# Six parts of 51, 62, 73, 73, 73 and 71 edge groups in place of 73, 73, 73, 73, 62 and 49, in a graph attention layer on one Trainium2 core

## The chip, the cores and the metric

The kernel runs on one NeuronCore of one Trainium2 chip. The metric is the device time of one execution in microseconds. Three runs of the kernel before gave 5107.2, 5124.87 and 5132.39 us, so the median is 5124.87 us. Engines are named as in the profile: PE (matrix engine), PEld (its weight loads), DVE (vector), ACT (scalar), POOL (GpSimd) and SP (which only issues DMAs here).

## The reference

The layer has 12,500 nodes with 128 features and 412,500 directed edges with 64 features each. `dst` is sorted; `src` is not.

```python
h = x @ Wn + bn
q = x @ Wq + bq; k = x @ Wk + bk; v = x @ Wv + bv
eh = edge_attr_64 @ We + be
attn_in = concatenate([q[src], k[dst], eh], -1)
hmid = leaky_relu(attn_in @ A1 + b1, 0.2)
scores = leaky_relu(hmid @ A2 + b2, 0.2)          # 8 heads
w = softmax(scores.mean(-1), axis=0)               # over all edges
out = segment_sum(w[:, None] * v[dst], src, num_segments=12500)
y = layernorm(h + out) * gamma + beta
return layernorm(x + y)
```

The first layer is linear, so its products are folded: each edge needs one row of a table from its source node (`q A1`), one from its destination (`k A1` and `v`), and the product of its own features.

## The kernel before, in words

**Groups, blocks, tiles.** The edges are cut in the order of `dst` into 403 groups of 1024 (8 tiles of 128). The nodes are dealt into 98 blocks of 128 by their number modulo 98, so that each block gets about the same number of edges as a source. The work has two halves. The first, `make` (L749), takes the edges in the order of `dst`, forms for each edge one record of 260 floats (the sum of the destination's row and the edge's product, the row of `v`, and the place of the source in its block), and scatters it to a row of a DRAM table `rtab` that belongs to the block of its source. The second, `sums_of` (L980), reads the records back block by block, adds the source's row, computes the scores, keeps a running maximum for the softmax, and adds up `w * v` for the block's nodes.

**Parts.** The 403 groups are cut into six parts by `CUTS` (L34): 73, 73, 73, 73, 62 and 49 groups. Each part has its own number of tiles of room per block (`plan.tiles`, L61): 7, 7, 7, 7, 6 and 5. Two tables `rtab` alternate. The loop at L1568 emits, for p from 0 to 6, the instructions of `make(p)` interleaved evenly with those steps of the sums that deal with part p - 1; in part 0 the tables of the nodes (`tables`, L1495) and the preparation of the edge lists (`later`, L1547) stand in the place of the sums, packed into the first nine tenths of the part (`n0`, L1575). After part 5 nothing is left to make: the sums of the last part run alone, and then `closing` (L1314) normalises the rows. The order of the instructions on each engine is the order in which this loop emits them, and each engine runs its own in order.

**make, for one group.** SP loads `eat` (edge features), `dstb` and `kvs` four groups ahead (`load`, L754). PE and DVE count how many earlier edges go to each block (L785 to L836), which gives each edge its row. PE forms the records of four tiles in one PSUM tile `pkv` (L854, L860); ACT moves them out into a tile `rec` (L871, L872; six buffers); POOL issues one indirect DMA per tile (L883), so eight per group. A `rec` buffer is free again when its four scatters have landed.

**Filling.** Rows of a block that no record reaches must hold zeros before they are read. `fill` (L513) yields pieces for both tables: in each block the rows from the least count that can be expected up to the table's room of seven tiles. `fill_piece` (L526) writes them on SP from an SBUF tile `empty` (L508). In part 0 the pieces of the first table stand before group 40 (`plan.gate`, L76), those of the second in the rest of the nine tenths: 44 pieces of 780 KB and 54 of 520 KB.

**sums_of.** A unit is two blocks of one part: 14, 12 or 10 tiles; there are 49 units a part. Each unit's work is dealt into numbered steps (L1273 to L1305), and step numbers decide the order of emission. A unit's hidden layer takes two steps for each four tiles (`nk`), from step `s0`; the next unit's `s0` is `2 * nk` later (L990), so 8 steps for a unit of 14 tiles and 6 for 12 or 10. `e` (L987) is 1 for units of 14 tiles: it puts one or more steps between a DMA, or an operation on one engine, and the next one that needs it (the spread of the sources' row `rowB`, L1062; `biased`, `leaky_scores`, `heads`, L1290 to L1292; `reference`, L1295). For units of 12 and 10 tiles `e` is 0. `load` (L1012) reads a unit's records into one of six buffers `rt`. `heads` allocates `psm` (two PSUM buffers), which is freed by `total` (L1251) of the unit two before. `starts[p]` is the step of the first load of part p; the loop emits the steps up to `starts[p] - HOLD` (7) in the part before (L1574).

Of the kernel before, what the change touches and what calls it, by code (L numbers as in the profile page):

```python
# [10 lines left out]
FP = mybir.dt.float32  # L11
# [9 lines left out]
P = 128  # L21
# [9 lines left out]
XA = 3  # L31
SPAN = 42
NP = 6
CUTS = 0, 0.1811, 0.3623, 0.5434, 0.7246, 0.8784, 1  # L34
TABS = 2
WIDTH = 14
HOLD = 7
LATE = 3
R = 4
WR = 260  # L40
# [3 lines left out]
class Plan:  # L44
# [4 lines left out]
    def __init__(self, n, e, nb, groups):  # L49
        self.n, self.e, self.nb, self.groups = n, e, nb, groups  # L50
        cut = [round(groups * c) for c in CUTS]
        self.parts = list(zip(cut[:-1], cut[1:]))
# [400 lines left out]
def sorted_path(  # L453
# [8 lines left out]
    nc = tc.nc  # L462
    nb = plan.nb
# [6 lines left out]
    dram = ctx.enter_context(tc.tile_pool(name="dram", bufs=1, space=DRAM))  # L470
# [31 lines left out]
        nc.vector.memset(headsum[32 * j : 32 * j + 32, j : j + 1], 1.0)  # L502


    fmax = max(max(f) for f in plan.fill)
    empty = None

    def empties(pool):  # L508
        nonlocal empty
        empty = pool.tile([P, fmax, WR], FP, name="empty")  # L510
        nc.vector.memset(empty, 0.0)

    def fill(k, n):  # L513

        cap = plan.cap
        b = 0
        while b < nb:
            m = 1
            while m < n and b + m < nb and plan.fill[k][b + m] == plan.fill[k][b]:
                m += 1  # L520
            f = plan.fill[k][b]
            if f:
                yield b, m, f
            b += m

    def fill_piece(k, b, m, f):  # L526
        cap = plan.cap
        piece = nc.sync.dma_start(
            out=rtab[k][b * cap : (b + m) * cap, :]
            .rearrange("(b c) w -> b c w", b=m)[:, cap - f * P : cap, :]  # L530
            .rearrange("b (p k) w -> p b (k w)", p=P),
            in_=empty[:, :f, :]
            .rearrange("p (o k) w -> p o (k w)", o=1)
            .to_broadcast([P, m, f * WR]),
        ).ins
        if k == 0:
            tc.declare_no_dep(piece, group="rows0", reason="rows that no record has reached")
            tc.add_to_no_dep_group("fill0", piece)

# [28 lines left out]
    with tc.tile_pool(name="prep", bufs=1) as prep, tc.tile_pool(  # L568
        name="pprep", bufs=1, space=PSUM
# [103 lines left out]
    def spans():  # L673

        lim = const.tile([P, 2], FP)
        for i, (op, most) in enumerate(((ALU.max, SPAN - 1.0), (ALU.min, 0.0))):
            nc.vector.tensor_reduce(lim[:, i : i + 1], mm[:, i, :], AX.X, op)
            sign = 1.0 if op == ALU.max else -1.0
            nc.vector.tensor_scalar(
                bad[:, i : i + 1], lim[:, i : i + 1], sign, -sign * most, op0=ALU.mult, op1=ALU.add  # L680
            )
# [16 lines left out]
        out=above, in_=above, compare_op=ALU.is_gt, fill=0.0, base=0,  # L698
# [281 lines left out]
    def sums_of(bp):  # L980


        plans, s0, first, free, done, starts = [], 19, None, [], [], {}
        for p, bs, t in units:
            nt = len(bs) * t
            nk = -(-nt // 4)
            L, e = 2 * nk, int(nk > 3)  # L987
            turn = 11 if e else 8
            if plans:
                s0 += 2 * plans[-1][1]  # L990


            load_at = free[-BLKS] + 1 if len(free) >= BLKS else 0
            lead = turn + 8 if p in starts or p == 0 else turn + 8 + LATE
            s0 = max(s0, load_at + lead - 1)
            if first is not None:
                s0 = max(s0, first - (L + 5 + 3 * e))
            if len(done) > 1:
                s0 = max(s0, done[-2] + 1 - (L + 4 + 2 * e))
            f = s0 + L + 5 + 3 * e  # L1000
            load_at = max(load_at, s0 - lead)
            free.append(f + 3 + e + L)
            done.append(f + 4 + e + L)
            first = f + L
            starts.setdefault(p, load_at)
            plans.append((nt, nk, s0, load_at, f, e, turn))
        steps = {}

# [264 lines left out]
        for i, (nt, nk, s0, load_at, f, e, turn_at) in enumerate(plans):  # L1273
# [7 lines left out]
            for k in range(nk):  # L1281
                c = 4 * k
                n, s = min(4, nt - c), s0 + 2 * k
# [15 lines left out]
            for j, t0 in enumerate(range(0, nt, 4)):  # L1299
                n = min(4, nt - t0)  # L1300
# [6 lines left out]
        closing(bp, do, tail, f + 3 + e, f + 5 + e + 2 * j + 4)  # L1307
        order = lambda at: [(fn, args) for _, fn, args in sorted(at, key=lambda x: x[0])]
        return [order(steps.get(s, [])) for s in range(max(steps) + 1)], [
            starts[p] for p in range(NP)  # L1310
        ]


    def closing(bp, do, s0, s1, s2):  # L1314
# [164 lines left out]
        for name, bufs in (("xq", 2), ("nq", 1), ("eq", 1))  # L1479
    )  # L1480
    empties(np_)

    def parts3(to, rest, half):
# [63 lines left out]
    def later():  # L1547

        for c in range(1, len(chunks)):
            yield from edges(tmp, c, CH // 2)  # L1550
            yield

    def covered():

        most = np_.tile([1, G], FP, name="most")
        g = 0
        while g < G:
            h = g
            while h < G and ready.get(h, ng) == ready.get(g, ng):
                h += 1  # L1560
            nc.vector.memset(most[:, g:h], float(3 * NB * P * ready.get(g, ng) - P))
            g = h
        nc.vector.tensor_tensor(most, start, most, op=ALU.subtract)
        nc.vector.tensor_reduce(bad[0:1, 2 + 2 * NP : 3 + 2 * NP], most, AX.X, ALU.max)

    with tc.manual_schedule():
        done = 0
        for p in range(NP + 1):  # L1568
            a = make(p) if p < NP else iter(())
            na = 6 * (plan.parts[p][1] - plan.parts[p][0]) if p < NP else 0  # L1570
            if p == 1:
                steps, starts = sums_of(pool("blk", BLKS))
            here = done
            until = 0 if p == 0 else starts[p] - HOLD if p < NP else len(steps)  # L1574
            n0 = na * 9 // 10  # L1575
            fills = []
            if p == 0:
                i0 = 0
                for k, i1 in enumerate((6 * plan.gate - 12, n0)):
                    pieces = list(fill(k, 2))  # L1580
                    fills += [
                        (i0 + (i1 - i0) * j // len(pieces), (k, *piece))
                        for j, piece in enumerate(pieces)
                    ]
                    i0 = i1
            fills = fills[::-1]
            tabs, made, nt = tables() if p == 0 else iter(()), 0, 1 + (2 * ng - 1) * (NB + 7)
            more, sent, ne = later() if p == 0 else iter(()), 0, 11 * (len(chunks) - 1)
            for i, _ in enumerate(a):
                while fills and fills[-1][0] <= i:  # L1590
                    fill_piece(*fills.pop()[1])
                while made < nt and made * n0 < i * nt:
                    next(tabs, None)
                    made += 1
                while sent < ne and sent * n0 < i * ne:
                    next(more, None)
# [90 lines left out]
```

## Time and profile before

The profiled execution took 5108.98 us; its span, from the first to the last instruction, is 5107.2 us.

| | busy us | share of the span |
|---|---|---|
| PE | 4197.8 | 82% |
| DVE | 3989.1 | 78% |
| POOL | 3347.9 | 66% |
| ACT | 3275.2 | 64% |
| PEld | 3121.7 | 61% |

These shares are means over stages with different contents, so the profile is best read by stage. The stages can be found without any mark in the program: L883 issues eight scatters per group, so a stretch that holds 8 x 73 = 584 of them is one part of 73 groups. By this count the parts of `make` run from 65 to 870, to 1640, 2407, 3174, 3878 and 4482 us; the sums of the last part run until about 4975 us, and the closing until 5107 us. A stage's table gives, for each engine, the busy time in the stretch and in brackets the number of instructions; PEclk is the granted clock as a share of the full one, and then follow the busy share of the 16 DMA engines and the rate.

### The profile page before, as it was taken

Reading aid. Unit: us, or ns where it says so; the run is one execution under the profiler, and the core shown is the slowest. Engines: PE = TensorE matmul, PEld = TensorE weight load, DVE = VectorE, ACT = ScalarE, POOL = GpSimd, SP = SyncE. Lnnn points to the kernel's source line nnn. Section 1 sums busy time; section 2 is a strip of 40 time slices with the busy share of each in tenths; the row PEclk is TensorE's granted clock in tenths of the full one; section 3 lists DMA queues with packets and bytes.
Section 4 is the critical chain, followed back from the end, with each engine's and each line's share of the span. In section 5 each row is a group of like instructions: output and inputs, shape, how many; then the busy total and the mean of one; then the engine's idle time right before and its main releaser. Section 6 shows DMA issues by size and latency. Waiting matters only on the chain.

```text
span 5107.2 us, 97900 instructions
## 1 busy us (share of the span) xinstructions
PE 4197.8 (82%) x32676; PEld 3121.7 (61%) x32676; DVE 3989.1 (78%) x10011; ACT 3275.2 (64%) x8487; POOL 3347.9 (66%) x3265
## 2 busy tenths in 40 slices
PE   4556564998998989998999998999999899988880
PEld 2333332666766767776766776677777676666660
DVE  7666663888887888888888887888888788766678
ACT  2333331666766777776777776777777677766776
POOL 3777777777777777777777777777767566611002
PEclk7666665999999999999999999999999999999995
DMA  5889895988888998998988998998998898878763
GB/s 188 281 277 314 292 336 175 323 297 296 298 302 278 316 316 308 316 304 297 322 310 306 314 314 286 315 318 311 318 316 301 291 307 305 293 248 265 247 232 139
DMA packets 589700, 1477.77 MB, mean 289 GB/s; under 512 B 102746, under 2 KB 315629, under 8 KB 587392
## 3 DMA queue, kind: packets, MB, share of 16 engines
q1 hardware_dynamic: 434224, 1042.03, 62.4%
q0 software_dynamic: 154752, 429.39, 22.0%
q8 instruction: 259, 4.24, 0.3%
q14 instruction: 257, 2.11, 0.1%
q10 hardware_dynamic: 208, 0.00, 0.0%
HBM read 890.36 MB, written 580.68 MB: 288 GB/s over the span
## 4 chain that ended last, share of the span: by engine, by line
DMA 35%; PE 19%; POOL 16%; DVE 14%; issue 9%; ACT 7%; SPq 1%; ACTq 0%; DVEq 0%; POOLq 0%
DMA rtab<-rec,idx 18%; POOL rtab L883 16%; DMA row<-slT 6%; DMA rt<-rtab 5%; PE psm L1246 4%; DMA rowB<-row 4%; PE ph L1094 3%; PE pkv L860 3%; ACT rec L871 2%; PE ph L1085 2%; ACT ohw L1217 2%; PE pkv L854 2%; DVE hm L1109 2%; PE psm L1155 2%; PE psc L1122 1%
## 5 line engine op out<-in xcount | busy, mean ns | idle before, releaser
L883 POOL DMA_INDIRECT rtab<-rec,idx x3224 | 3287.0, 1020 | 1190.9 <-issue 789.4
L871 ACT ACTIVATE rec<-pkv 128x1024 f32<-128x1024 f32 x806 | 821.6, 1019 | 1125.1 <-DMA rtab<-rec,idx 789.5
L1217 ACT ACTIVATE ohw<-ohs,w 128x128 f32<-128x128 bf16 x3822 | 1259.5, 400 | 13.2 <-PE psm L1246 1.4
L1246 PE MATMUL psm<-rt,ohw 128*128 128x128 f32 x7644 | 1150.3, 293 | 8.9 <-ACT ohw L1217 7.5
L1246 PEld LDWEIGHTS psm<-rt,ohw 128*128 128x128 f32 x7644 | 983.5, 198 | 104.2 <-ACT hm L1105 31.3
L1105 ACT ACTIVATE hm<-ph 128x512 f32<-128x512 f32 (+1 forms) x1078 | 583.4, 541 | 473.3 <-PE ph L1094 466.8
L854 PE MATMUL pkv<-kvs,ohd 128*128 128x256 bf16 x3224 | 550.0, 299 | 402.9 <-ACT rec L871 378.9
L1094 PE MATMUL ph<-ohT,qs 128*128 128x512 bf16 (+3 forms) x4116 | 819.6, 321 | 39.6 <-DVE ohT L1074 39.4
L1109 DVE TENSOR_TENSOR hm<-ph,hm 128x512 f32<-128x512 f32 (+1 forms) x1078 | 668.0, 620 | 114.9 <-ACT hm L1105 114.5
L860 PE MATMUL pkv<-WeS,eat 64*128 64x128 f32 x6448 | 658.7, 329 | 0.0
L854 PEld LDWEIGHTS <-ohd 128*128 128x128 bf16 x3224 | 321.8, 105 | 542.2 <-issue 453.1
L1085 PE MATMUL ph<-ident,rt 128*128 128x128 f32 x3822 | 622.5, 281 | 14.3 <-DVE hm L1109 13.5
L1074 DVE TENSOR_SCALAR ohT<-rowB,iotaP 128x512 bf16<-128x512 uint8 (+1 forms) x1078 | 521.8, 484 | 119.3 <-DMA rowB<-row 114.3
L860 PEld LDWEIGHTS pkv<-WeS,eat 64*128 64x128 f32 x6448 | 487.9, 213 | 201.1 <-issue 199.0
L1094 PEld LDWEIGHTS <-qs 128*128 128x128 bf16 x4116 | 395.3, 100 | 173.4 <-issue 50.8
L1085 PEld LDWEIGHTS ph<-ident,rt 128*128 128x128 f32 x3822 | 477.2, 152 | 22.5 <-DVE hm L1109 17.9
L823 DVE TENSOR_TENSOR ats<-pc,oh 128x792 f32<-128x792 f32 x403 | 392.3, 973 | 106.1 <-PE pc L805 103.5
L1203 DVE TENSOR_TENSOR ohs<-iotaE,sl 128x512 bf16<-128x512 bf16 (+1 forms) x1078 | 415.0, 385 | 51.2 <-ACT ohw L1217 50.3
L1155 PE MATMUL psm<-headsum,z 128*128 128x4 f32 (+1 forms) x2156 | 286.4, 254 | 146.0 <-DVE z L1145 65.7
L834 DVE TENSOR_REDUCE pos<-ats 128x8 f32<-128x792 f32 x403 | 389.9, 967 | 3.4
L1155 PEld LDWEIGHTS psm<-headsum,z 128*128 128x128 f32 (+1 forms) x2156 | 273.9, 198 | 176.9 <-DVE z L1145 79.1
L1122 PE MATMUL psc<-hm,A2s 128*32 128x512 f32 (+3 forms) x2352 | 319.5, 533 | 12.8 <-DVE slT L1053 7.0
(151 smaller groups left out, 4080.8 us busy)
## 6 DMA issues: line engine op xcount, KB each, us to landing
rt<-rtab SPq DMA_DIRECT2D x196, 1820.0 KB
eat<-in_ea SPq DMA_DIRECT2D x201, 512.0 KB
rt<-rtab SPq DMA_DIRECT2D x49, 1560.0 KB
rt<-rtab SPq DMA_DIRECT2D x49, 1300.0 KB
qs<-qtab SPq DMA_DIRECT2D x294, 192.0 KB
rtab<-rec,idx POOLq DMA_INDIRECT x3224
dstb<-dtab SPq DMA_DIRECT2D x201, 256.0 KB
rowB<-row SPq DMA_DIRECT2D x196, 224.0 KB
```

What stands on the lines that cost most here:

```text
L854: nc.tensor.matmul(pk[:, h, i, :], ohd[:, t * P : (t + 1) * P], kvs, start=(i == 0), stop=False,)
L860: nc.tensor.matmul(pk[:, h, i, :D], eat[h * DE : (h + 1) * DE, (j + i) * P : (j + i + 1) * P], WeS[h * DE : (h + 1) * DE, :], start=False, ...
L871: nc.scalar.activation(rec[:, :, :, : 2 * D], pk, AF.Copy)
L883: one_tile = nc.gpsimd.indirect_dma_start(out=rtab[p % TABS][:, :], out_offset=bass.IndirectOffsetOnAxis(ap=idxs[g][:, t : t + 1], axis=0) ...
L1074: nc.vector.tensor_scalar(st["oh"][k][:, : n * P], st["rowB"][:, t0 * P : (t0 + n) * P], iotaP, None, op0=ALU.is_equal,)
L1085: nc.tensor.matmul(ph[:, j * P : (j + 1) * P], st["rt"][:, t0 + j, :D], ident, is_transpose=True, start=(j == 0), stop=False,)
L1094: nc.tensor.matmul(ph[:, cols], st["qs"][:, j0 // t, s, :], oh[:, cols], start=False, stop=(s == 2 and j1 == t0 + n),)
L1105: nc.scalar.activation(hm, state[i]["ph", k][:, : n * P], AF.Copy, scale=SLOPE)
L1109: nc.vector.tensor_tensor(hm, ph[:, : n * P], hm, op=ALU.max)
L1155: nc.tensor.matmul(st["psS"][:, t0 + j : t0 + j + (nv - 1) * sw + 1 : sw], z[: 32 * nv, j * P : (j + 1) * P], headsum[: 32 * nv, :nv], sta ...
L1217: nc.scalar.activation(ohw[:, j, :], ohs[:, :, j], AF.Copy, scale=st["w"][:, t0 + j : t0 + j + 1])
L1246: nc.tensor.matmul(st["psS"][:, (1 + u) * P : (2 + u) * P], ohw[:, j, :], st["rt"][:, t0 + j, D : 2 * D], start=(k == 0), stop=(k == t - 1),)
```

## The change

The parts become 51, 62, 73, 73, 73 and 71 groups, with room for 5, 6, 7, 7, 7 and 7 tiles per block; both the number of tiles (3822) and that of the units (294) stay. In part 0 the fill now covers each table only up to the room of the part that uses it first (two tiles per block and table: 98 pieces of 520 KB). The rows above are zeroed while the sums of that part are read: in part 1 two tiles per block of the first table (49 pieces of 520 KB), in part 2 one tile per block of the second (49 pieces of 260 KB). These late pieces are copied from a small DRAM tensor `zeros`, since `empty` lies in a pool that is closed after part 0; `zeros` is written once at the start. Units of 12 and 10 tiles get `e = 1` and eight steps when they are not of the last part, and their sources are turned 12 steps ahead rather than 8. The steps of a part end at the larger of `starts[p] - HOLD` and one past the last load of the part before.

```diff
-CUTS = 0, 0.1811, 0.3623, 0.5434, 0.7246, 0.8784, 1
+CUTS = 0, 0.1266, 0.2804, 0.4615, 0.6427, 0.8238, 1
...
+    zeros = dram.tile([P, fmax, WR], FP, name="zeros")
...
         nc.vector.memset(empty, 0.0)
+        nc.sync.dma_start(out=zeros, in_=empty)
...
     def fill(k, n):
-        cap = plan.cap
-        b = 0
+        b, top = 0, plan.tiles[k]
         while b < nb:
...
-            f = plan.fill[k][b]
-            if f:
-                yield b, m, f
+            a = plan.cap // P - plan.fill[k][b]
+            if a < top:
+                yield b, m, a, top - a
             b += m
 
+    def fill_top(k, n):
+        top, most = plan.tiles[k], plan.cap // P
+        if top < most:
+            for b in range(0, nb, n):
+                yield b, min(n, nb - b), top, most - top
...
-            .rearrange("(b c) w -> b c w", b=m)[:, cap - f * P : cap, :]
+            .rearrange("(b c) w -> b c w", b=m)[:, a * P : (a + f) * P, :]
...
-            in_=empty[:, :f, :]
+            in_=(empty if source is None else source)[:, :f, :]
...
-            L, e = 2 * nk, int(nk > 3)
-            turn = 11 if e else 8
+            L, e = 2 * nk, int(nk > 3 or p < NP - 1)
+            turn = (11 if nk > 3 else 12) if e else 8
             if plans:
-                s0 += 2 * plans[-1][1]
+                s0 += 2 * plans[-1][1] if not plans[-1][5] else max(8, 2 * plans[-1][1])
...
             starts.setdefault(p, load_at)
+            ends[p] = load_at
...
-            starts[p] for p in range(NP)
+            max(starts[p] - HOLD, ends[p - 1] + 1) if p else 0 for p in range(NP)
...
-            until = 0 if p == 0 else starts[p] - HOLD if p < NP else len(steps)
+            until = 0 if p == 0 else starts[p] if p < NP else len(steps)
...
+            if 0 < p <= TABS:
+                pieces = list(fill_top(p - 1, 2))
+                fills = [
+                    (na // 8 + na * j // (2 * len(pieces)), (p - 1, *piece, zeros))
+                    for j, piece in enumerate(pieces)
+                ]
```

More of the change, by code (lines that the diff above doesn't have):

```diff
@@ L502, in sorted_path @@
         nc.vector.memset(headsum[32 * j : 32 * j + 32, j : j + 1], 1.0)
-    fmax = max(max(f) for f in plan.fill)
+    fmax = max(
+        max(plan.tiles[k] - plan.cap // P + max(plan.fill[k]), plan.cap // P - plan.tiles[k])
+        for k in range(TABS)
+    )
+    zeros = dram.tile([P, fmax, WR], FP, name="zeros")
     empty = None
@@ L520, in fill, with fill_piece @@
                 m += 1
-            f = plan.fill[k][b]
-            if f:
-                yield b, m, f
+            a = plan.cap // P - plan.fill[k][b]
+            if a < top:
+                yield b, m, a, top - a
             b += m
-    def fill_piece(k, b, m, f):
+    def fill_top(k, n):
[3 more added lines that the diff above has]
+                yield b, min(n, nb - b), top, most - top
+    def fill_piece(k, b, m, a, f, source=None):
         cap = plan.cap
@@ L535, in fill_piece @@
         ).ins
-        if k == 0:
+        if k == 0 and source is None:
             tc.declare_no_dep(piece, group="rows0", reason="rows that no record has reached")
@@ L980, in sums_of @@
     def sums_of(bp):
-        plans, s0, first, free, done, starts = [], 19, None, [], [], {}
+        plans, s0, first, free, done, starts, ends = [], 19, None, [], [], {}, {}
         for p, bs, t in units:
```

## The prediction

> **What bounds the kernel now.** The page comes first: no engine is busy throughout, so shares of the whole say little.
>
> ```profile
> span 5107.2 us, 97900 instructions
> PE 4197.8 (82%) x32676; PEld 3121.7 (61%) x32676; DVE 3989.1 (78%) x10011; ACT 3275.2 (64%) x8487; POOL 3347.9 (66%) x3265
> ```
>
> The second view is the table of stretches, cut where the count of POOL instructions reaches eight per group (584 is 73 groups; two or so at an edge are counted twice).
>
> ```profile
> core 0: us, PE busy (x) PEld busy (x) DVE busy (x) ACT busy (x) POOL busy (x), PEclk, DMA share, GB/s
> 0.00:65.00 65.00, 12.77 (x44) 9.21 (x44) 40.58 (x81) 2.41 (x3) 2.95 (x14) 0.66 0.30 93
> 65.00:870.00 805.00, 457.51 (x2452) 298.24 (x2453) 503.82 (x960) 265.50 (x377) 620.19 (x584) 0.65 0.82 279
> 870.00:1640.00 770.00, 690.64 (x5600) 515.19 (x5600) 630.98 (x1508) 517.69 (x1345) 591.85 (x584) 0.94 0.88 299
> 1640.00:2407.00 767.00, 700.90 (x5763) 530.43 (x5762) 648.91 (x1590) 552.28 (x1464) 588.69 (x586) 0.96 0.90 310
> 2407.00:3174.00 767.00, 701.01 (x5763) 528.78 (x5761) 649.72 (x1593) 553.17 (x1466) 588.97 (x585) 0.96 0.90 309
> 3174.00:3878.00 704.00, 661.17 (x5374) 498.91 (x5371) 595.49 (x1495) 524.88 (x1403) 500.48 (x497) 0.96 0.91 314
> 3878.00:4482.00 604.00, 553.30 (x4506) 415.13 (x4506) 472.18 (x1207) 427.98 (x1169) 396.58 (x392) 0.97 0.88 300
> 4482.00:4975.00 493.00, 420.46 (x3184) 325.86 (x3184) 335.08 (x1061) 350.29 (x1047) 29.14 (x14) 0.95 0.75 246
> 4975.00:5107.00 132.00, 0.00 (x0) 0.00 (x0) 112.36 (x520) 81.00 (x216) 29.02 (x14) 0.50 0.40 147
> ```
>
> Stages 0 to 5 last 805, 770, 767, 767, 704 and 604 us, the sums that run alone ("the tail") 493, the closing 132. The three stages of 73 groups with sums take 767/73 = 10.5 us a group. The grouped lines of POOL for stages 0, 2 and 4, and for the last tenth of stage 0, say why:
>
> ```profile
> L883 POOL DMA_INDIRECT rtab<-rec,idx x584 | 620.5, 1062 | 246.1 <-issue 155.8 <-DMA rtab<-empty 61.4 <-DMA rtab<-rec,idx 13.4
> L883 POOL DMA_INDIRECT rtab<-rec,idx x586 | 590.1, 1007 | 178.6 <-issue 142.3 <-DMA rtab<-rec,idx 10.1 <-ACT ohw L1217 7.3
> L883 POOL DMA_INDIRECT rtab<-rec,idx x497 | 501.1, 1008 | 203.8 <-issue 110.6 <-ACT rec L872 53.3 <-ACT ohw L1217 9.8
> L883 POOL DMA_INDIRECT rtab<-rec,idx x81 | 80.4, 992 | 24.7 <-issue 20.1 <-DMA rtab<-rec,idx 4.3 <-ACT rec L871 0.3
> ```
>
> In stage 2 POOL is in a scatter for 590 us and, between two, in "issue" for 142: 732 of 767 us, 95%. In stage 0 it is 776 of 805. So POOL sets the pace in stages 0 to 3. In stage 4 the sum is 612 of 704 (87%), and POOL waits 53 us for ACT's records: there PE, busy 661 of 704 (94%), sets it. In the tail PE is busy 420 of 493 (85%) with nobody else in its way. The kernel thus has three regimes: POOL by groups, PE with sums and groups, and sums alone.
>
> **The change part by part.** *Stage 0* loses 22 groups and keeps the tables. The stretch in which it has only groups gives their bare price, and the stretch before it shows the load with tables:
>
> ```profile
> 65.00:765.00 700.00, 414.09 (x2202) 269.67 (x2203) 467.01 (x876) 244.49 (x341) 539.83 (x503) 0.67 0.88 299
> 765.00:870.00 105.00, 43.41 (x252) 28.57 (x251) 36.81 (x85) 21.02 (x37) 80.36 (x81) 0.50 0.43 145
> ...
> 665.00:765.00 100.00, 61.64 (x320) 39.82 (x319) 64.51 (x131) 31.23 (x50) 77.33 (x75) 0.67 0.98 336
> ```
>
> 105 us / 81 x 8 = 10.37 us a group, so 805 - 22 x 10.37 = 577 us. This keeps whole the time that the tables add to the scatters. The mean scatter is 1062 ns in stage 0 and 992 ns without tables; were that surcharge proportional to the groups, the stage would be 805 x 51/73 = 562 us. The Trainium skill (SBUF — State Buffer, "Who interferes with whom") says that a VectorE operation in a two-port mode shuts GpSimd out of the shared ports until it ends; by that rule the surcharge belongs to the table operations and stays whole, which speaks against the change by 15 us, and the two means agree with it.
>
> Then the transfers. The issues, with the software queue's total:
>
> ```profile
> q0 software_dynamic: 154752, 429.39, 22.0%
> ...
> rt<-rtab SPq DMA_DIRECT2D x49, 1300.0 KB
> qs<-qtab SPq DMA_DIRECT2D x294, 192.0 KB
> ...
> eat<-in_ea SPq DMA_DIRECT2D x201, 512.0 KB
> ...
> dstb<-dtab SPq DMA_DIRECT2D x201, 256.0 KB
> ...
> atab<-part SPq DMA_DIRECT2D x294, 128.0 KB
> rtab<-empty SPq DMA_DIRECT2D x44, 780.0 KB
> ...
> rtab<-empty SPq DMA_DIRECT2D x54, 520.0 KB
> kvs<-kvtab SPq DMA_DIRECT2D x403, 64.0 KB
> ...
> rowB<-row SPq DMA_DIRECT2D x49, 160.0 KB
> ```
>
> A group moves 429.39/403 + 0.262 + 0.131 + 0.066 = 1.524 MB. The 700 us at 299 GB/s are 209 MB: 63 groups 96, fills 64, so tables and edge lists 49. After the change the same nine tenths hold 46 groups (70 MB), fills of 98 x 520 KB (52 MB) and the 49: 171 MB in 577 - 54 = 523 us, 327 GB/s. The busiest 100 us above moved 336 at a share of 0.98, with no fewer scatters (75). I take 322, hence 531 + 54 = 585 us; the bounds are 577 and, at the old mean of 299, 626.
>
> *Stage 1*: 62 groups cost POOL 62 x 10.5 = 651 us. PE's part is far below: the tail's 420/558 = 0.753 us a tile (row below) gives 369 for 490 tiles, and stages 2 and 4, which differ by 11 groups, give (700.9 - 661.2)/11 = 3.6 a group, so 223 more. Transfers: 94 MB for groups, 65 of `rt`, 10 of `qs`, 8 of `rowB`, 6 of `atab`, and the late fill of 26: 210 MB. At the 314 GB/s of stage 4 that is 669. I take 665. No row shows a copy from DRAM to DRAM: at the best the fill lies under the rest (651), at the worst it counts twice (236/0.314 = 752); the nearest row, the fill from SBUF, counts once. SP issues 49 more DMAs there in order, each in front of some load of `eat`, `dstb` or `kvs`, but those run four groups, 42 us, ahead.
>
> *Stage 2*: 73 groups at 10.5 are 767 us (bounds 757, at the bare price, and 775): its late fill of 13 MB is what its units read less, 98 tiles of 133 KB, so its traffic is that of a stage of before, and PE has those 98 tiles less. *Stages 3 and 4* are what stages 2 and 3 were: 767 each. *Stage 5* has 71 groups where it had 49: 71 x 10.5 = 746 (bounds 740 and 760).
>
> Writing `zeros` is one more DMA at the start; I cost it at nothing, since SP sits there anyway until DVE has the first rows of the tables:
>
> ```profile
> SPq L589 <- DVE skv L584: 20.3, 1, 20.3
> ```
>
> The eight steps for small units cost nothing by themselves: steps are dealt evenly over a part's groups, and POOL's 10.5 us a group covers them. The shorter hold (4 and 5 steps for 7 before the first loads of parts 1 and 2) lengthens this wait of SP:
>
> ```profile
> SPq L1016 <- DMA rtab<-rec,idx: 74.7, 4, 32.6
> ```
>
> One wait is 32.6 us, the other three 14 each; three more steps of 2 us leave them below the 42 us (four groups) of prefetch: nothing; 10 us if that cover is gone.
>
> *The tail.* ACT weighs each tile once, so its count gives the tiles that it holds; PE's waits in the tail, and in stage 4, where nearly all units have `e = 1`, follow:
>
> ```profile
> L1217 ACT ACTIVATE ohw<-ohs,w 128x128 f32<-128x128 bf16 x558 | 185.0, 399 | 4.4 <-PE psm L1246 1.4
> ```
> ```profile
> PE psm L1155 <- DVE z L1145: 44.7, 49, 2.5
> PE ph L1094 <- DVE ohT L1074: 15.0, 14, 2.2
> ```
> ```profile
> PE psm L1155 <- DVE part L1262: 27.4, 23, 7.0
> ```
>
> 558 tiles are the 490 of the part and 68, 5.7 units, still in the pipeline. Units of 14 make that 686 + 79 = 765. PE is busy 0.753 us a tile: 576 us. Of its idle 72 us, 45 are one wait per unit for `z` that `e = 1` gives a step more; stage 4 does not list it. In its place comes the wait for `psm`, 27 us for 49 units, so 30 for 55; with the 15 for `ohT` that is 621 us. Bounds: 576, and 765 x 493/558 = 676 if a tile costs what it does now.
>
> Sum: 65 + 585 + 665 + 767 + 767 + 767 + 746 + 621 + 132 = 5115 us against the span of 5107. The execution's own time is 1.8 above its span and 16 below the median of the runs, so 5133; I say 5130.
>
> **The rivals.** *Faster: PE fills the tail.* If the waits vanish (576) and transfers do not hold stages 0 and 1 (577, 651), the sum is 5115 - 45 - 8 - 14 = 5048, on the median's scale 5066. For it: stage 4 runs PE at 94%; against: that stage has 399 steps of the schedule, 1.76 us each, the tail 337 of 1.46, which leaves each chain less time.
>
> *Slower: transfers hold the small stages.* Where stages 0 and 1 get no more than 299 GB/s, they take 626 and 702: +78, so 5211. It decides once the DMA share reaches its ceiling before POOL does; SP's loads then come late and ACT waits for PE instead of for scatters. For it: 327 GB/s were never held for 500 us. Against: 336 once, unharmed. The Trainium skill (DMA: Bandwidth & Descriptors, "Specifications") gives a limit of some 358 GB/s of HBM per core, by which, as an estimate, neither stage would be held; no row here reaches it.
>
> *Slower: the tail keeps its price a tile*: 676, so +55 and 5188. For it: a step would hold as many tiles as now, 765/444 against 558/337 (1.7), and once one wait goes the next in line may last as long. Against: the wait for `z` is the largest by far and has a named cause.
>
> *The change does not shorten stage 0*, because the tables' own chain between PE, DVE and ACT paces its first 700 us: 754 in place of 585, 5302. Against it stands this wait, POOL's queue reaching back to ACT:
>
> ```profile
> ACT rec L871 <- DMA rtab<-rec,idx: 398.0, 93, 9.8
> ```
>
> **How the numbers follow.** Forecast 0.45, PE fills the tail 0.26, transfers 0.14, the tail's old price 0.11, the tables' chain 0.04. The forecast's own range is 5095 to 5170; the whole reaches from 5055 to 5225. A change of 0.5%, 25 us, is about what a measurement of this kernel can tell from none. The forecast gives 0.08 to faster, 0.28 to same and 0.09 to slower; the faster rival 0.24 to faster and 0.02 to same; the three slower ones 0.03 to same and 0.26 to slower. In all 0.32, 0.33 and 0.35.
>
> **What would show it.** Eight scatters a group again mark the stages: 408 by about 650 us, 496 more by 1315, then 767, 767, 767 and 746. A stage 0 over 620 with a DMA share above 0.95 is the rival of transfers; with a lower share and DVE waiting for PE it is the tables' chain. In the tail the wait of L1155 for `z` should be gone and PE busy above 90%; a tail above 660 proves that step wrong. Scatters in stages 1 and 2 much faster than 10.37 us a group would overthrow POOL as the bound.

## The result and the profile after

The changed kernel took 5057.33 us (median of four runs, 5054.13 to 5064.48), the kernel before 5128.63 us beside it (four runs, 5107.2 to 5134.36). The ratio is 0.9882, with a 95% interval of 0.9865 to 0.99: 1.2% faster. The forecast of 5130 us, no change, was wrong: the time lies at the low end of the whole range, where the faster rival stood.

A repeat in a later session (`c2_changed_again` below) gave 0.9887 (0.986 to 0.9914). In three of the later sessions every kernel, the one before too, took 18 to 20% longer, and in the one of them that had the changed kernel (`c1_changed_again`, expected at 0.988) the change gained nothing, 1.0055 (1.0037 to 1.0074); the text below uses of them mainly the tails, which with the closing took what they took elsewhere to within about 6 us (688.8 us in c1 against 688.4 here).

The profiled execution took 5054.13 us. Its page, the same two lines as before:

```profile
span 5052.4 us, 98033 instructions
PE 4182.9 (83%) x32676; PEld 3101.9 (61%) x32676; DVE 4003.6 (79%) x10011; ACT 3266.3 (65%) x8487; POOL 3352.2 (66%) x3265
```

Nothing in them tells where the 55 us went: the busy times of both kernels agree to within two thirds of a per cent. The table of stretches, cut again by eight scatters a group, does. Columns as in the prediction: the stretch, its length, the busy time and count of PE, PEld, DVE, ACT and POOL, the granted clock, the share of the DMA engines, GB/s.

```profile
0.00:64.00 64.00, 11.94 (x44) 8.62 (x44) 40.06 (x81) 2.41 (x3) 2.66 (x14) 0.68 0.30 97
64.00:590.00 526.00, 316.26 (x1712) 206.79 (x1712) 401.42 (x757) 207.96 (x271) 404.52 (x367) 0.73 0.97 327
590.00:644.00 54.00, 21.36 (x125) 14.11 (x124) 16.48 (x48) 10.15 (x18) 41.21 (x43) 0.50 0.38 135
644.00:1316.00 672.00, 566.08 (x4524) 416.00 (x4524) 511.64 (x1292) 409.07 (x1077) 504.46 (x496) 0.91 0.93 312
1316.00:2084.00 768.00, 657.61 (x5215) 483.84 (x5215) 577.93 (x1401) 475.94 (x1266) 590.00 (x585) 0.93 0.92 307
2084.00:2852.00 768.00, 701.21 (x5722) 528.29 (x5722) 645.01 (x1581) 549.21 (x1452) 589.72 (x586) 0.94 0.91 310
2852.00:3619.00 767.00, 701.57 (x5761) 528.29 (x5759) 651.42 (x1595) 554.08 (x1467) 589.05 (x584) 0.96 0.91 309
3619.00:4365.00 746.00, 691.70 (x5669) 522.89 (x5667) 631.84 (x1560) 550.76 (x1466) 572.11 (x568) 0.96 0.91 311
4365.00:4920.00 555.00, 515.13 (x3912) 393.07 (x3912) 415.16 (x1178) 425.58 (x1256) 29.41 (x14) 0.98 0.77 266
4920.00:5053.00 133.00, 0.00 (x0) 0.00 (x0) 112.61 (x521) 81.09 (x216) 29.02 (x14) 0.50 0.40 147
```

Set beside the sum of the prediction (us):

| | before | forecast | after |
|---|---|---|---|
| head | 65 | 65 | 64 |
| stage 0 | 805 | 585 | 580 |
| stage 1 | 770 | 665 | 672 |
| stages 2 and 3 | 1534 | 1534 | 1536 |
| stage 4 | 704 | 767 | 767 |
| stage 5 | 604 | 746 | 746 |
| tail | 493 | 621 | 555 |
| closing | 132 | 132 | 133 |

Seven of the eight rows are met to within 7 us; the tail is 66 us short of its forecast. Between before and after, stages 0 and 1 give 323 us, stages 4 and 5 take back 205 and the tail 62.

The groups of POOL's scatters in 64:590, 644:1316 and 1316:2084 (line, tiles and count; busy time and mean ns; idle time before them and what ended it):

```profile
L894 POOL DMA_INDIRECT rtab<-rec,idx x367 | 405.0, 1104 | 182.2 <-issue 97.3 <-DMA rtab<-empty 60.7 <-DVE first L629 8.3
L894 POOL DMA_INDIRECT rtab<-rec,idx x496 | 504.8, 1018 | 167.8 <-issue 116.4 <-ACT rec L883 12.7 <-DMA rtab<-rec,idx 8.4
L894 POOL DMA_INDIRECT rtab<-rec,idx x585 | 590.9, 1010 | 178.3 <-issue 148.4 <-ACT ohw L1229 7.9 <-DMA rtab<-rec,idx 7.3
```

POOL still sets the pace in stages 0 to 3. The scatters beside the tables now take 1104 ns instead of 1062: fewer of them, and each longer. Against the bare 992 ns the surcharge is (1104 - 992) x 367 = 41 us here, and was (1062 - 992) x 584 = 41 us before. It goes with the tables, as the prediction had it, and the records' start and end times say with which operation: 92 of the 408 scatters of stage 0 overlap a `less` (L1503, a tensor_tensor of DVE that belongs to the tables) and take 1422 ns in the mean, 42 us in all over the median of 961 ns; before it was 91 of 584 at 1414 ns, again 41 us. The 62 that overlap no DVE operation take 959 ns.

The tail: ACT's weighing, which counts the tiles, and the waits of PE (line waited for; us in total, times, longest):

```profile
L1229 ACT ACTIVATE ohw<-ohs,w 128x128 f32<-128x128 bf16 x734 | 241.2, 399 | 2.0 <-DVE ohs L1215 0.3
```
```profile
PE psm L1167 <- DVE part L1274: 17.6, 10, 13.2
PE ph L1097 <- DVE hm L1121: 15.0, 15, 2.1
PE psm L1258 <- ACT ohw L1229: 1.6, 3, 0.6
```

The wait for `z` (44.7 us before) is gone, as said; PE is busy 515 of 555 us, 93%. What stands in its place is not quite what was said: of the 17.6 us for `psm` one wait of 13.2 is most, and `hm` stands where `ohT` was. The tail holds 734 tiles where 765 were forecast, and PE is busy 515.13/734 = 0.702 us a tile where before it was 0.753.

### The profile page after: what moved, and what is told of

Same layout as the page of the kernel before. It is cut to its first block, busy times and chain, and to the rows that moved or that the text cites. A ratio compares the mean times of both kernels' runs of the same rounds, so it can differ in the third digit from the quotient of the medians.

```text
span 5052.4 us, 98033 instructions
## 1 busy us (share of the span) xinstructions
PE 4182.9 (83%) x32676; PEld 3101.9 (61%) x32676; DVE 4003.6 (79%) x10011; ACT 3266.3 (65%) x8487; POOL 3352.2 (66%) x3265
## 4 chain that ended last, share of the span: by engine, by line
DMA 35%; PE 23%; DVE 17%; POOL 11%; ACT 7%; issue 7%; SPq 1%; ACTq 0%; DVEq 0%; POOLq 0%
DMA rtab<-rec,idx 16%; POOL rtab L894 11%; DMA rt<-rtab 9%; PE psm L1258 5%; DMA row<-slT 4%; PE ph L1106 4%; DMA rowB<-row 3%; PE pkv L871 3%; PE ph L1097 3%; ACT rec L882 2%; PE psc L1134 2%; DVE hm L1121 2%; ACT ohw L1229 2%; PE pkv L865 2%; PE psm L1167 2%
## 5 line engine op out<-in xcount | busy, mean ns | idle before, releaser
L1258 PEld LDWEIGHTS psm<-rt,ohw 128*128 128x128 f32 x7644 | 997.2, 200 | 59.2 <-ACT ohw L1229 17.7
L1106 PE MATMUL ph<-ohT,qs 128*128 128x256 bf16 (+3 forms) x4116 | 818.7, 320 | 0.0
L865 PE MATMUL pkv<-kvs,ohd 128*128 128x256 bf16 x3224 | 529.5, 291 | 229.4 <-ACT rec L882 212.1
L871 PE MATMUL pkv<-WeS,eat 64*128 64x128 f32 x6448 | 634.8, 320 | 0.0
L871 PEld LDWEIGHTS pkv<-WeS,eat 64*128 64x128 f32 x6448 | 468.6, 205 | 190.8 <-issue 186.6
L1215 DVE TENSOR_TENSOR ohs<-iotaE,sl 128x512 bf16<-128x512 bf16 (+1 forms) x1078 | 430.0, 399 | 48.2 <-ACT ohw L1229 46.6
L1134 PE MATMUL psc<-hm,A2s 128*32 128x512 f32 (+3 forms) x2352 | 341.5, 545 | 77.9 <-DVE slT L1065 75.0
```

Of the source, the lines that this page charges most:

```text
L865: nc.tensor.matmul(pk[:, h, i, :], ohd[:, t * P : (t + 1) * P], kvs, start=(i == 0), stop=False,)
L871: nc.tensor.matmul(pk[:, h, i, :D], eat[h * DE : (h + 1) * DE, (j + i) * P : (j + i + 1) * P], WeS[h * DE : (h + 1) * DE, :], start=False, ...
L1106: nc.tensor.matmul(ph[:, cols], st["qs"][:, j0 // t, s, :], oh[:, cols], start=False, stop=(s == 2 and j1 == t0 + n),)
L1258: nc.tensor.matmul(st["psS"][:, (1 + u) * P : (2 + u) * P], ohw[:, j, :], st["rt"][:, t0 + j, D : 2 * D], start=(k == 0), stop=(k == t - 1),)
```

## The experiments

Times are medians, stages and waits are those of the profiled run; "tail and closing" is what lies between the end of the last scatter and the end of the span: 625.9 us before, 688.4 after. In the diffs the lines taken out are those of the changed kernel.

**e1_tail_e0: the last part without the added step.** Is it the step that makes the tail cheap, or the size of its units alone? The row of the sources is asked for two steps later as well.

```diff
-            L, e = 2 * nk, int(nk > 3 or p < NP - 1)
-            turn = (11 if nk > 3 else 12) if e else 8
+            L, e = 2 * nk, int(p < NP - 1)
+            turn = (11 if nk > 3 else 12) if e else 9
```

> The changed kernel with e = 0 for the units of the last part alone (still 14 tiles and 8 steps; the sources are turned 9 steps ahead instead of 11). Theory A, the added step makes the tail cheap: without it PE waits again about 0.9 us a unit for z, so the tail goes from 555 to about 600 us (590 to 650), the span from 5052 to about 5100, and PE's idle time in the tail from 40 to 85 us. Theory B, the size of the unit makes it cheap (fewer matmuls a tile): the tail stays within 555 +- 10 us and PE's busy time a tile at 0.70 us.

5124.4 us, ratio to before 1.0028 (1.0015 to 1.004); stages 0 to 5 as in the changed kernel (584, 672, 769, 769, 768, 747), tail and closing 751.0. The tail's stretch, then waits of PE and DVE in it:

```profile
4373.00:4988.00 615.00, 531.19 (x3891) 401.02 (x3891) 415.55 (x1159) 436.34 (x1249) 29.70 (x14) 0.93 0.68 239
```
```profile
PE ph L1106 <- DVE ohT L1086: 53.9, 34, 2.6
...
PE psm L1167 <- DVE z L1157: 2.9, 3, 1.3
```
```profile
DVE ohT L1086 <- DMA rowB<-row: 72.7, 36, 15.9
```

The step and the earlier row together are worth 63 us, the whole gain of the change. But the wait that came back is not the one for `z`: PE waits for `ohT`, DVE for the spread of the sources' row from DRAM. That points to a DMA asked for too late; whether it is the larger part, the next run tells.

**e9_tail_e0_turn11: the same with the row asked for as early as in the changed kernel**, which parts the two (the diff is against e1).

```diff
-            turn = (11 if nk > 3 else 12) if e else 9
+            turn = (11 if nk > 3 else 12) if e else 11
```

> As e1_tail_e0 (e = 0 in the last part), with the sources turned 11 steps ahead as in the changed kernel, so that the row rowB is on its way two steps earlier than in e1_tail_e0. Theory A1, the tail's gain is the earlier row: PE's 54 us of waiting for ohT go, the tail is 560 to 580 us and the whole within 20 us of the changed kernel. Theory A2, it is the step between operations of different engines: the waits move to z and ref, the tail stays near 615 us and the whole near 5115.

Ratio 1.0108 (1.0085 to 1.0131) where the changed kernel itself had 1.0055 in its session. Tail and closing 728.7 against 688.8 for the changed kernel beside it (c1) and 751.0 for e1 in the other session: of 62 us, 40 belong to the added step and, across the sessions, 22 to the earlier row. That lies between the two theories, and the late DMA was the smaller part. The waits of PE say what the 40 are:

```profile
PE ph L1106 <- DVE ohT L1086: 23.9, 30, 1.8
PE psc L1058 <- DVE sl L1050: 13.1, 13, 3.8
PE psm L1167 <- DVE z L1157: 7.6, 7, 1.3
```

Three waits on DVE, none of them large; together 45 us. Against c1 PE's idle time is 23 us longer, and PE is also busy 14 us longer with as many matmuls (539.7 against 525.3).

**e2_old_parts and e3_old_parts_tail_e1: the new steps with the old parts.** e2 keeps everything of the change but the sizes; e3 gives the last part's units of 10 tiles the added step and eight steps as well.

```diff
-CUTS = 0, 0.1266, 0.2804, 0.4615, 0.6427, 0.8238, 1
+CUTS = 0, 0.1811, 0.3623, 0.5434, 0.7246, 0.8784, 1
...
-            L, e = 2 * nk, int(nk > 3 or p < NP - 1)
+            L, e = 2 * nk, 1
```

(the second pair of lines in e3 alone)

> The changed kernel with the cuts of before (73, 73, 73, 73, 62, 49), so that only its steps differ from before: units of 12 take eight steps with e = 1 in stage 5, units of 10 in the tail keep six and e = 0. If the gain comes from the cuts: the kernel before within 0.5% (5090 to 5130 us), tail 493. If the steps give a part of it: stage 5 goes from 604 to 585 us or less, the whole to about 5090.

> As e2_old_parts, and the last part's units of 10 tiles also take eight steps with e = 1. Theory A (the added step): the tail goes from 493 to about 450 us, 40 less than in e2_old_parts. Theory B (the size of the unit): the tail stays within 10 us of it, or grows, since 49 units take 8 steps instead of 6.

e2: 5126.36 us, 1.0031 (1.0018 to 1.0043). e3: 5127.47 us, 1.0029 (1.0015 to 1.0043). The steps without the parts gain nothing; they cost 16 us. In both, stage 5 (49 groups beside units of 12 tiles, bound by PE) takes 626 and 629 us instead of 604: where POOL does not cover them, the new steps cost some 20 us, though eight tiles fewer are left for the tail (550 for 558). The tail and closing are 641.0 and 626.9; but e2's profile is of its slowest run (5145.34 us), and by the medians, 1 us apart, the added step in e3's tail gains nothing. The tail of e3, its tiles and its waits:

```profile
4501.00:4993.00 492.00, 440.90 (x3154) 330.41 (x3154) 344.16 (x1036) 339.29 (x1035) 29.15 (x14) 0.95 0.71 239
```
```profile
L1229 ACT ACTIVATE ohw<-ohs,w 128x128 f32<-128x128 bf16 x550 | 181.4, 398 | 4.8 <-DVE ohs L1215 3.1
```
```profile
PE psm L1258 <- ACT ohw L1229: 28.3, 54, 2.0
PE psc L1134 <- DVE slT L1065: 9.6, 14, 1.8
PE psm L1167 <- DVE z L1157: 5.3, 8, 1.8
```

The wait for `z` has fallen from 44.7 to 5.3 us, and yet a tile costs 492/550 = 0.895 us, against 493/558 = 0.884 before. For units of 10 tiles the prediction's third rival gives the right price, but its reason is half of it: the next in line (`ohw`, 28.3 us) takes part of the place, PE's idle time still falls from 72 to 51 us, and PE's busy time grows by as much, from 420.46 to 440.90, with 30 matmuls fewer (140 ns each for 132). Why they take longer is not shown. So neither the step nor the wait for `z` alone makes a tile cheap.

**e11_last_62: units of 12 tiles in the tail.** Parts of 49, 73, 73, 73, 73 and 62 groups, all units with the added step: does a tile's price fall with the unit's size?

```diff
-CUTS = 0, 0.1266, 0.2804, 0.4615, 0.6427, 0.8238, 1
+CUTS = 0, 0.1216, 0.3027, 0.4839, 0.665, 0.8462, 1
...
-            L, e = 2 * nk, int(nk > 3 or p < NP - 1)
+            L, e = 2 * nk, 1
```

> Parts of 49, 73, 73, 73, 73 and 62 groups, each with the added step. Stage 0 about 559 us, stages 1 to 4 about 767 each, stage 5 (62 groups beside 14-tile units) about 704, and a tail of units of 12 tiles. Theory A (a tile's price in the tail falls with the unit's size as well as with the added step: 0.88 us at 10, 0.75 at 14): about 0.81 a tile, tail and closing about 647, span 5030 to 5050. Theory B (only the added step counts, 0.75 a tile): tail and closing about 610, span about 5000. Theory C (12 tiles behave as 10 do, 0.88): tail and closing about 690, span about 5090.

The whole (6091.66 us, 1.0065, 1.0046 to 1.0085, in one of the three sessions named with the result) says nothing of the expected spans; the tail does. The second row is the tail of the changed kernel in c1:

```profile
5432.00:5960.00 528.00, 491.62 (x3513) 368.51 (x3511) 352.79 (x1003) 368.07 (x1108) 30.59 (x14) 0.98 0.73 250
```
```profile
5365.00:5922.00 557.00, 525.34 (x4019) 400.82 (x4016) 429.97 (x1209) 438.64 (x1297) 30.26 (x14) 0.99 0.77 268
```
```profile
L1229 ACT ACTIVATE ohw<-ohs,w 128x128 f32<-128x128 bf16 x664 | 216.6, 399 | 3.7 <-PE psm L1258 1.1 <-DVE ohs L1215 0.8
```
```profile
L1229 ACT ACTIVATE ohw<-ohs,w 128x128 f32<-128x128 bf16 x756 | 248.3, 399 | 2.1 <-DVE ohs L1215 0.3
```

528/664 = 0.795 us a tile, between 0.895 and 0.756, near theory A's 0.81; tail and closing took 663 us, 16 more than A said, since more tiles were left than its 647 us hold at 0.81 (636). With the added step throughout, the three sizes read as follows (tiles and us from the rows above; a unit is 10, 12 or 14 tiles):

| | tiles | units | us a tile | us a unit | PE busy a unit | PE matmuls a unit |
|---|---|---|---|---|---|---|
| e3, 10 tiles | 550 | 55.0 | 0.895 | 8.95 | 8.02 | 57.3 |
| e11, 12 tiles | 664 | 55.3 | 0.795 | 9.54 | 8.89 | 63.5 |
| after, 14 tiles | 734 | 52.4 | 0.756 | 10.59 | 9.83 | 74.6 |
| c1, 14 tiles | 756 | 54.0 | 0.737 | 10.31 | 9.73 | 74.4 |

The tail after has a gap of 13.2 us that c1's has not (more on it below), so c1 is the better row for 14 tiles. From 10 tiles to 14 a unit grows by 1.36 us, 0.34 a tile; a line through these two sizes leaves, as an estimate, some 5.5 us of a unit that do not depend on its tiles. PE's busy time grows alike (0.43 a tile). A tail is some 52 to 55 units long whatever their size, and tiles added to them are cheap.

**e4_fill_all_in_0: the whole fill in part 0.** The new parts, but the upper rows are filled in part 0 as before.

```diff
-        max(plan.tiles[k] - plan.cap // P + max(plan.fill[k]), plan.cap // P - plan.tiles[k])
+        max(plan.fill[k])
...
-        b, top = 0, plan.tiles[k]
+        b, top = 0, plan.cap // P
...
-        top, most = plan.tiles[k], plan.cap // P
+        top, most = plan.cap // P, plan.cap // P
```

> The changed kernel with every row filled in part 0, as before (91 MB there instead of 52, none later). If transfers hold stage 0 (share 0.97 at 327 GB/s): 39 MB more at 330 GB/s are +118 us there, stage 1 falls from 672 to about 651, the whole rises by about 95 us to 5150. If POOL sets its pace and SP's queue is hidden: stage 0 stays at 580 to 600, stage 1 falls to 651, the whole falls to about 5040.

5111.8 us, 0.9997 (0.9986 to 1.0009): 649 us in stage 0 (580), 656 in stage 1 (673), tail and closing 7 us longer (695.6), the rest equal. Without the later fill the change would have gained nothing. The stretches and a wait of POOL show the transfers at their limit:

```profile
64.00:664.00 600.00, 324.67 (x1696) 211.01 (x1695) 398.21 (x753) 206.74 (x269) 400.17 (x370) 0.69 1.00 353
664.00:714.00 50.00, 24.99 (x144) 16.25 (x143) 20.45 (x55) 12.40 (x22) 38.12 (x40) 0.50 0.41 140
714.00:1369.00 655.00, 553.34 (x4524) 407.93 (x4524) 513.17 (x1292) 406.38 (x1077) 503.09 (x496) 0.92 0.86 280
```
```profile
POOL rtab L894 <- ACT rec L883: 114.1, 25, 62.1
```

The DMA engines stand at 1.00 for 600 us, and POOL waits for records 52 us beyond the first long wait (62.1), which every part 0 begins with. This is the second rival, made to happen: it decides here at 353 GB/s, and the 327 of the changed kernel's stage 0 did not hold POOL up. The stage came out shorter than expected because the ceiling was put at 330. The Trainium skill (DMA: Bandwidth & Descriptors, "Specifications") has some 358 GB/s of HBM per core. These 353 GB/s, held for 600 us, lie near it, but it is no ceiling for a short time: 100 us of the changed kernel's stage 0 moved more (the row below), and POOL kept its pace. Whether the DMA engines (share 1.00) or the memory held e4 is not shown.

```profile
464.00:564.00 100.00, 62.57 (x338) 41.58 (x340) 74.03 (x156) 33.77 (x51) 77.32 (x74) 0.75 1.03 363
```

**e7c_fill_spread: the late fill over 7/8 of the part instead of 1/2.** For the 21 us by which stage 1 lies above the 651 of POOL alone.

```diff
-                    (na // 8 + na * j // (2 * len(pieces)), (p - 1, *piece, zeros))
+                    (na // 16 + na * 7 * j // (8 * len(pieces)), (p - 1, *piece, zeros))
```

> The changed kernel with the late pieces spread over 15 sixteenths of parts 1 and 2. If crowded transfers cost stage 1 its 21 us over POOL's 651: stage 1 takes 655 to 662 and the whole is 10 to 17 us below the changed kernel, 0.985 of the kernel before. If not: 0.988 of it.

5040.5 us, 0.9867 (0.9838 to 0.9897); the changed kernel beside it, **c2_changed_again**, 5047.08, 0.9887.

> The changed kernel once more beside these: 0.988 of the kernel before, a span near 5052 us, tail and closing together 687 us as in both profiles so far.

Only stage 1 differs: 656 us against 669.5 (672.7 in the first session). By the medians the whole is 6.6 us shorter, by the two profiled runs 14; 10 to 17 were expected. The first row below is its stage 1; the two after it are from the changed kernel's (first session): 200 us in which the late fill is issued, and the 200 before them, into which it begins:

```profile
644.00:1300.00 656.00, 558.53 (x4477) 413.71 (x4526) 510.18 (x1292) 408.78 (x1077) 504.30 (x496) 0.92 0.93 320
```
```profile
844.00:1044.00 200.00, 168.71 (x1306) 124.76 (x1306) 147.01 (x373) 118.27 (x314) 141.59 (x141) 0.89 0.97 340
644.00:844.00 200.00, 153.78 (x1197) 110.69 (x1197) 137.75 (x343) 107.90 (x275) 153.07 (x152) 0.87 0.95 322
```

Where the late fill is issued, at 340 GB/s in the mean, POOL issues 141 scatters in 200 us instead of 152. Spreading the pieces thins the transfers and SP's order alike, so which of the two costs the 14 us is not separated; the slowest 50 us (844 to 894, 33 scatters) moved 309 GB/s, no more than elsewhere. This is the fastest of all versions by its median, but its interval overlaps that of c2.

**e6c_late_fill_twice: each late piece is written twice**, so 26 MB and 13 MB more in stages 1 and 2; the values written are the same.

```diff
                     for j, piece in enumerate(pieces)
+                    for _ in range(2)
```

> The changed kernel with every late piece issued twice (26 MB more in stage 1, 13 MB more in stage 2). Stage 1 takes 672 us where POOL alone would take 651. If transfers cost these 21 us: 690 to 730 in stage 1, 775 to 790 in stage 2. If the 21 us are the first unit's wait for scatters to land or something else: stage 1 within 5 us of 672.

5398.93 us, 1.0584 (1.0554 to 1.0614): stage 1 takes 867.6 us and stage 2 912.2. As a test of the transfers it failed, since the share of the DMA engines fell (0.81 in stage 1). SP's waits say why:

```profile
SPq L539 <- DMA rtab<-zeros: 358.9, 50, 10.5
```

The second write of the same rows waits on SP until the first has landed, about 7 us each time, and all loads behind it in SP's order wait along. The pieces of the change itself stand in the same queue without such a wait. It shows the price of a waiting instruction there: some 200 us for 50 of them.

**e5c_old_steps: the new parts with the old steps** for units of 10 and 12 tiles, so `e = 0` and six steps.

```diff
-            L, e = 2 * nk, int(nk > 3 or p < NP - 1)
-            turn = (11 if nk > 3 else 12) if e else 8
+            L, e = 2 * nk, int(nk > 3)
+            turn = 11 if e else 8
...
-                s0 += 2 * plans[-1][1] if not plans[-1][5] else max(8, 2 * plans[-1][1])
+                s0 += 2 * plans[-1][1]
```

> The changed kernel with the steps of before (six, e = 0) for units of 12 and 10 tiles, in stages 1 and 2. If POOL's 10.5 us a group covers whatever the sums do there: 672 and 768 us again, 0.988 of the kernel before. If the added step keeps their waits off the path: 30 us or more above, 0.994 or higher.

5051.52 us, 0.9895 (0.9868 to 0.9922); stages 0 to 2 take 581, 668 and 768. The eight steps of small units neither cost nor gain beside POOL, as forecast.

**The other runs of the three sessions named with the result**, against before in the same session: the changed kernel (c1) 1.0055 (1.0037 to 1.0074), the old steps (e5, e5b) 1.0005 and 1.0019, the spread fill (e7, e7b) 1.0029 and 1.0033, the pieces twice (e6) 1.0315, and two kernels that stretch the tables over 24/25 of part 0 instead of 9/10. One is e8, with nothing else changed; the other is e10, with the spread fill too.

```diff
-            n0 = na * 9 // 10
+            n0 = na * 24 // 25
```

> The changed kernel with the tables, the edge lists and the second fill spread over 24 of 25 parts of part 0 instead of nine tenths. If POOL sets the pace of stage 0 and the tables add a fixed sum to its scatters (41 us in both kernels): no change, within 8 us of 5057. If the crowding of transfers or of DVE costs there: 10 to 20 us less.

> The change with the late fill spread over the whole part (as in e7c) and the first fill of part 0 stretched by shortening the zeroed rows' share to 24/25. Theory A (stage 0 is set by POOL's scatters and a fixed surcharge of the tables): stage 0 stays at about 580 us, stage 1 falls to about 656 as in e7c, median about 5040. Theory B (stage 0 also pays for crowding of the fill): stage 0 falls by 10 to 15 us, median about 5028.

In the traces of these sessions (e6 aside) stage 0 takes 9 to 11% longer than the same stage elsewhere, stages 1 to 5 take 21 to 31%, and the tail with the closing, which has no groups, 1% at most. In c1 a group costs 13.1 to 13.4 us in each of the stages 1 to 5 (12.4 in stage 0), and in stage 3 POOL is in scatters or issue for 731 of 967 us and waits 136 us for ACT's records. So POOL is not the bound there, and a group costs as much in the stage that it goes to as in the one that it leaves, which would explain why moving it gains nothing. This is argued, since the kernel before has no trace in those sessions; what slows the stages is not shown.

e8: 1.0024, its stage 0 644.3 us, to the tenth that of the old steps beside it (644.3): no effect. e10: 1.0034 (1.0012 to 1.0055), stage 0 627.9 us beside 628.6 of e11, which has two groups fewer; since POOL does not set the pace there, what e8 and e10 would give where it does stays open.

## Why the prediction was wrong

**Stage 0** (585 forecast, 580 measured) was right with its reasons: 22 groups at the bare price (805 - 226 = 580; 22 x 10.37 = 228), the tables' surcharge kept whole at 41 us, and 327 GB/s in the first 526 us, to the digit the rate that the working gave. The value taken, 322, was 8 us too careful. That the surcharge goes with VectorE's operations fits those 41 us in both kernels, but the rule that the prediction quotes, on two-port modes, is not the one that fits `less`: the Trainium skill (SBUF — State Buffer, "Who interferes with whom") says that a tensor_tensor has no such mode, and that a VectorE operation with two inputs in SBUF contends with a GpSimd instruction that reads SBUF. The 1422 ns beside `less`, against 959 beside no DVE operation, agree with that; no run leaves `less` out.

**Stage 1** (665, 672) is POOL's 651 and some 20 us where the late fill is issued, most of which e7c takes away. The sum through 314 GB/s gave 669, nearer than the reason deserved, which was luck: the stage moved 312, but e7c's moved 320.

**Stages 2 to 5** were right to 2 us: POOL's 10.5 us a group. The late fill of stage 2 and the eight steps cost nothing there (e5c); e2 and e3 show that the steps cost some 20 us in a stage that POOL does not cover.

**The tail** (621, 555) is the step that failed, in the words "Units of 14 make that 686 + 79 = 765. PE is busy 0.753 us a tile: 576 us." The wait for `z` went, as forecast. The sum then fails by 66 us: 38 by the price of a tile, 23 by the number of tiles and 5 by PE's idle time. The last two hang together:

- *The price* (38 us: 734 x (0.753 - 0.702)). PE has 3184/558 = 5.71 matmuls a tile with units of 10 tiles and 3912/734 = 5.33 with units of 14, at 132 ns each in both (420.46/3184 and 515.13/3912). Part of a unit's matmuls does not grow with its tiles, and a price per tile from small units carries it along. Both rows for that, x3184 and x558, stood in the prediction; the size of the unit was not divided out. The 132 ns are no constant: e1 has 137 and e3 and e11 have 140, for reasons that are not shown.
- *The tiles and the idle time* (23 us: 31 x 0.753; and 5). When POOL sets the pace, its queue is behind ACT's records. The last record leaves ACT, and the last scatter POOL, at these times in the changed kernel and in the one before (start, duration, engine, line, operation, tiles):

```profile
4338.03 1.00 ACT L882 ACTIVATE rec<-pkv 128x1024 f32<-128x1024 f32 x1
4363.05 0.96 POOL L894 DMA_INDIRECT rtab<-rec,idx  x1 [0.30 <-issue]
```
```profile
4474.89 1.02 ACT L871 ACTIVATE rec<-pkv 128x1024 f32<-128x1024 f32 x1 [0.75 <-PE pkv L860]
4480.32 0.96 POOL L883 DMA_INDIRECT rtab<-rec,idx  x1 [0.30 <-issue]
```

 25 us against 5: while POOL works off its queue, the sums go on, and fewer tiles are left for the tail. Every trace with units of 14 tiles in the last part agrees: 730 or 734 tiles where the last scatter ends 23 to 26 us after the last record, 756 to 762 where it ends 5 to 6 after. So 22 to 28 of the 31 tiles go with this queue. But it did not shorten the tail. The first records of the last part can only be loaded when its scatters have landed; SP waits for that, DVE for the load, PE for DVE:

```profile
SPq L1028 <- DMA rtab<-rec,idx: 18.9, 1, 18.9
```
```profile
4372.72 0.18 DVE L1050 SCALAR_TENSOR_TENSOR sl<-mask,rt 128x14 bf16<-128x14 bf16 x1 [14.40 <-DMA rt<-rtab]
```
```profile
4374.07 1.87 PE L1167 MATMUL psm<-headsum,z 128*128 128x4 f32 x8 [13.16 <-DVE part L1274]
```

 In c1 the queue is 6 us long, this gap is missing, and 756 tiles took 557 us, as long as 734 did. There the 64 us between 621 and 557 are 44 of price (756 x (0.753 - 0.695)), 7 of tiles and 13 of idle time, so the price is the larger part in both. That the idle time met its forecast (40 for 45) was luck: without the gap the waits for `psm` are 4.4 us, and 6.3 in c1, for the 30 forecast, the 15 for `ohT` are gone, and the 13 to 15 for `hm` were not in the sum.

38 + 23 + 5 are the 66 us. Put right, the sum is 5115 - 66, and 4 more from the small differences of the other rows: 5053, where the last stretch ends.

**The rivals.** "PE fills the tail" gave 5066 us and came nearest (5057), by another way: it needed PE to wait for nothing, and PE waits nearly as long as forecast but has less to do. "The tail keeps its price a tile" is wrong for 14 tiles and, by e3, right for 10. "Transfers hold the small stages" is what e4 shows, at 353 GB/s; the changed kernel's stage 0 moved 327. The tables' chain did not show. The chance of 0.32 for faster fell on this one term: an error of 66 us in it is more than twice the 25 us that part faster from the same.

**What gained.** 33 groups left stages 0 and 1, where each costs POOL about 10 us, for stages 4 and 5. There PE was the bound, and POOL had idle time: 63 us for 11 groups (5.7 each) and 142 for 22 (6.5 each, in which the larger units that stage 5 now sums are counted too). 323 - 205 = 118 us, of which the longer tail takes 62. The later fill is what lets stage 0 give its share (by e4 62 us of the span: 5114.1 - 5052.4), and the added step and the earlier row are what keeps the longer tail at 62 us instead of 125 (e1).

## What to carry to other kernels

Price what is moved in the stage that it leaves and in the stage that it goes to: a group cost 10.4 us where its engine was the bound and about 6 where another one was. Never scale a stage by tiles when part of its work comes once per unit; count instructions per unit and per tile, and fit the price from two sizes. A scheduling step that frees one wait is worth something only if the next wait in line is shorter, which depends on the size of the unit: here it gained 40 us at 14 tiles (e9 against c1) and none at 10 (e3). And a stage that hands over early is not a gain when the next one needs its last piece: the 20 us that the sums had ahead of POOL's queue came back in good part as a gap of 13.

## What was not expected of the hardware

The DMA engines held 353 GB/s for 600 us at a share of 1.00, and 363 GB/s at 1.03 for 100 us with POOL still busy 77 of 100. A write that has to wait for an earlier one of the same rows cost about 7 us of SP's order each, and stage 1 some 200 us in all (e6c). One kind of DVE operation, `less`, carries nearly the whole surcharge of the scatters in stage 0: 1422 ns beside it, 959 beside no DVE operation.
